# Graph attention on one core: building the kept keys with one-hot matmuls and picking flagged queries with multiply and add, in place of indirect transfers

## The chip, the cores and the metric

The kernel runs on one core of a Trainium2 chip. The metric is the device time in microseconds (us); the kernel before has a median of 13151.83 us over three runs (13146.24 to 13156.08). A core has these engines: PE (TensorE: matmul, with PEld its weight loads), DVE (VectorE), ACT (ScalarE), POOL (GpSimd) and SP (SyncE, which here only issues transfers). Each engine runs its own instructions strictly in the order written, and waits on semaphores for what others make.

## The reference, cut to what matters

Two layers on 3327 nodes with 128 features, with a sparse weighted adjacency matrix `adj` (about 0.12% of the entries plus the diagonal).

```python
# layer 0
x = layernorm(x + norm_rows(adj) @ x @ W_in + norm_rows(adj.T) @ x @ W_out)
# layer 1: d = 128 "heads" of h = 8 numbers each
q = (x @ Wq.T).reshape(d, n, h); k = ...; v = ...
a = einsum('dnh,dmh->dnm', q, k) * d**-0.5
a = a + adj + adj
a = softmax(a, axis=2)
out = einsum('dnm,dmh->dnh', a, v).reshape(n, h * d) @ Wo.T
x = layernorm(x + out)
```

So there are 128 attention maps of 3327 by 3327, each with only 8 numbers per query and key. The softmax needs, for every query of every head, a bound on its largest score.

## The kernel before, in words

**Stages.** Layer 0 takes until about 430 us of the span. The projections (L546 to L604) then write queries, keys and values of all heads to memory, with queries and keys split into bf16 parts, and the squared length of every key (`size_d`) and query (`reach_d`); they end at 1002 us. After a lead-in the main loop runs from 1097 to 12973 us, and a last phase (`last(joined)`) joins the parts, multiplies by Wo and normalizes.

**The main loop.** There are 32 groups of 4 heads (`GH`). A group walks over 7 blocks of up to 512 queries, and in each over 26 tiles of 128 keys. One step of this walk is called a half here: PE makes scores for one tile of keys, one block of queries and two heads (`e_ps`, L1156, two matmuls), ACT exponentiates all 1024 columns in one instruction (`es`, L1173; L1175 in the last, narrow block, for four heads at once), and, a step later, PE multiplies with the values (`o`, L1107). A group has 338 halves, the kernel 10,816. A program order written out by hand (a manual schedule for PE, ACT, DVE, Pool and SP) puts one piece of side work into each half. The two score banks `e_ps` and seven buffers `es` let PE and ACT run a little ahead of each other.

**Side work 1, the items.** The stream `maxima` yields items in a fixed order; the function `due(halves)` says how many must have been taken by a half, from a line drawn per group so that they are done `MARGIN` = 45 halves ahead of the next group's beginning. A half with an item is called busy. What the items find for group g + 1 while group g runs is the bound of each query's largest score:
- Only long keys can give a large score. For each head the 1024 longest keys (`TOP`), and the next 1024 up to `KEPT` = 2048, are compacted into `k_kept`, with their six bf16 part rows on partitions.
- `of_top(g, x)` (52 items for a pair of heads, x = 0 or 1): PE multiplies a tile of queries with 512 kept keys (L912) for both heads, DVE takes the maximum over the 512 (L921).
- `fix(g, x)` then compares, per query, the best found with query length times the longest key not looked at (`reach` from L711, L719). For each partition it lists up to `ROOM` = 8 queries that are not settled (`slots`), fetches their rows with 16 indirect gathers of 128 rows each on Pool's queue (L742), and splits them into bf16 parts on Pool.
- `of_rest(g, x)` (18 items) turns these rows (`slot_rows_q`, transposed by PE at L897) and multiplies them with the second 1024 kept keys. `merge` joins both maxima; `to_queries` turns the result (L868) and SP stores it (L871, L875) where the group's `q_e` loads read it.
- `turn()` moves the running `fix` and `merge` one step on, once per item.

**How the kept keys are built.** `select` finds, per head, the two length limits by halving, then ranks the keys with matmuls of ones and triangles, and computes for every key its place: 0 to 1023, 1024 to 2047, or a place behind all of these. `scatter` writes each group's 4 x 26 columns of 128 keys with one indirect transfer each (L518, 3328 in all, on Pool's queue, paced by the counter `load_of_pool`) into `kept_d`. `parts_of_kept` (L627 to L646) loads them back and splits them on Pool (`parts`, L640 to L645). Eight fill items per group transpose the parts on PE (L897, eight matmuls of 128 columns) and DVE casts them into `k_kept` (L906, 48 x 512).

**Side work 2, the neighbours (`beside`).** A half without an item, from the half `START` = 1536 on, runs one step of `neighbours()`. For each of 26 tiles of 128 nodes it makes the attention part of the nodes' own neighbours (up to 16 slots). K phase: for each slot a gather of 128 rows of all heads' keys (`near_rows`, L961, 4 KB a row, up to three ahead, four buffers), a product with the query on DVE in two halves (L996), a reduction (L999) and an addition. Then the softmax over the 16 slots: Pool subtracts the maximum (L1032), ACT exponentiates in four pieces (L1038), Pool multiplies by `gain` (L1041) and sums in four additions (L1043 to L1046). V phase: for each slot a gather, a product on DVE in two halves (`prod`, L1056), and Pool adds it to `acc` (L1062); a slot takes four steps. `prod` has two buffers that the K phase, the sums and the V phase share.

**Choices.** The selection of heads 0 to 3 and of 4 to 31 runs beside the projections, together with the scatters of group 0; the selections of the other heads run in halves without an item from `READY` = 310 on. The lead-in, before the first half, takes 8 fill items and 49 (`LEAD`) items of block maxima alone.

Of the kernel before, what the change touches and what calls it, by code (L numbers as in the profile page):

```python
# [11 lines left out]
U32 = mybir.dt.uint32  # L12
# [44 lines left out]
SLACK = 1.001  # L57
EARLY = [(0, 4), (4, 28)]
# [3 lines left out]
MARGIN = 45  # L62
# [7 lines left out]
def gnn_layers(ctx: ExitStack, tc: tile.TileContext, x, adj, adjt, w_in, w_out, wq, wk, wv, wo, out):  # L70
# [17 lines left out]
    nc.gpsimd.iota(order, pattern=[[-P, NT]], base=N - 1, channel_multiplier=-1)  # L88
    behind = const.tile([P, NT], F32, name="behind")
    nc.vector.tensor_copy(behind, order)  # L90
    every_f = const.tile([P, P], F32, name="every_f")
    nc.gpsimd.memset(every_f, 1.0)
    nothing = const.tile([1, HEADS], F32, name="nothing")
    nc.gpsimd.memset(nothing, 0.0)
# [3 lines left out]
    base_i = const.tile([P, 2, ROOM], I32, name="base_i")  # L98
    nc.gpsimd.iota(base_i, pattern=[[N, 2], [0, ROOM]], base=-P, channel_multiplier=1)
    query_base = const.tile([P, 2, ROOM], F32, name="query_base")  # L100
    nc.vector.tensor_copy(query_base, base_i)
# [25 lines left out]
    place_d = {  # L127
        first: dram.tile([P, n // GH, NT, GH], U32, name=f"place_d{first}") for first, n in EARLY + LATE
    }
    kept_d = [dram.tile([NP, H], F32, name=f"kept_d{h}") for h in range(HEADS)]  # L130
# [24 lines left out]
    with ExitStack() as c0:  # L155
# [145 lines left out]
        early = c_att.enter_context(tc.tile_pool(name="early", bufs=1))  # L301
        load = c_att.enter_context(tc.tile_pool(name="load", bufs=2))
# [87 lines left out]

        k_st = [with_ones(early.tile([P, 2, NP], BF16, name="k_st0"))]

        def select(pool, bank, first, n, tag=""):
# [3 lines left out]
            sizes = pool.tile([P, n, NT], F32, name=f"sizes{tag}")  # L397
# [4 lines left out]
            nc.sync.dma_start(sizes[P - 1 :, :, NT - 1], nothing[:, :n])  # L402
# [27 lines left out]
            for which, kept, bound in ((0, TOP, 3.3), (1, KEPT, 1.63)):  # L430
# [3 lines left out]
                for _ in range(HALVINGS):  # L434
# [4 lines left out]
                    nc.vector.tensor_scalar(few[:, 0], total, float(kept), None, op0=ALU.is_le)  # L439
                    nc.vector.tensor_scalar(few[:, 1], total, float(kept), None, op0=ALU.is_gt)  # L440
# [7 lines left out]
            for limit, to in ((0, top_least), (1, least)):  # L448
                nc.vector.tensor_scalar(to[:, first : first + n], limits[:, limit], SLACK, None, op0=ALU.mult)
            passed = [pool.tile([P, 2, n], BF16, name=f"passed{i}{tag}") for i in range(2)]  # L450
            nc.vector.memset(passed[0], 0.0)
            batch = min(NT, NB // n)
            by_tile = sizes.rearrange("p h t -> p t h")
            for t0 in range(0, NT, batch):
# [3 lines left out]
                masks = pool.tile([P, 2, nt, n], BF16, name=f"masks{tag}")  # L458
                for which in range(2):
                    nc.vector.tensor_tensor(  # L460
                        masks[:, which], by_tile[:, these], limits[:, which, None, :].to_broadcast(shape), op=ALU.is_gt
                    )
                    yield
                chosen = pool.tile([P, 2, nt, n], U32, name=f"chosen{tag}")
                nc.vector.tensor_copy(chosen[:, 0], masks[:, 0])
                nc.vector.tensor_sub(chosen[:, 1], masks[:, 1], masks[:, 0])
# [11 lines left out]
                ranks = [r.rearrange("p (t h) -> p t h", h=n) for r in ranks]  # L478
                second = pool.tile(shape, F32, name=f"second{tag}")
                place = pool.tile(shape, F32, name=f"place_of{tag}")  # L480
                nc.vector.tensor_tensor(second, leading[:, None, :].to_broadcast(shape), ranks[0], op=ALU.subtract)
                nc.vector.tensor_copy(place, ranks[0])
                yield
                nc.vector.tensor_add(second, second, ranks[1])
# [991 lines left out]
```

## Time and profile before

| | us |
|---|---|
| median of three runs | 13151.83 |
| the profiled execution | 13224.05 |
| its span | 13222.4 |
| PE busy in it | 11302.4 (85%) |
| ACT busy | 10990.5 (83%) |
| DVE busy | 9504.1 (72%) |
| POOL busy | 7295.3 (55%) |
| main loop with neighbours | 3094 to 10675 |
| main loop after them, with items | 10675 to 12638 |
| main loop without items | 12638 to 12973 |

A group line of the profile reads: line, engine, operation, output<-inputs, shapes, count | busy us, mean ns of one | idle time of the engine just before, and what ended it. A wait line reads: engine, instruction <- what it waited for: us in total, times, longest. An engine's busy share is an average over stages, so the stages are read one by one.

### The profile page before, as it was taken

The page shows a single profiled execution, that of the slowest core. Times are in us where ns is not written, and L with a number is a line of the kernel's source. Part 1 is how long each engine was busy: PE and PEld are TensorE (multiplying, and loading weights), DVE is VectorE, ACT ScalarE, POOL GpSimd, SP SyncE. Part 2 cuts the span into 40 slices and gives each one's busy share as a digit, 9 for nine tenths or more (in the row PEclk, how much of TensorE's full clock was granted, in tenths as well). Part 3 has the DMA queues.
Part 4 walks back from the last instruction along what each step waited for, and adds up shares of the span by engine and source line. Part 5 has one row for each costly group of instructions (what it writes and reads, how often), then busy time and mean ns, then how long its engine had stood idle before and what let it go on. Part 6 is the DMA issues. An engine that isn't in the chain of part 4 may idle for free.

```text
span 13222.4 us, 227945 instructions
## 1 busy us (share of the span) xinstructions
PE 11302.4 (85%) x84312; PEld 2645.3 (20%) x84312; DVE 9504.1 (72%) x16699; ACT 10990.5 (83%) x11667; POOL 7295.3 (55%) x6732
## 2 busy tenths in 40 slices
PE   7537877998898898888989889889899889999986
PEld 3211111211111111111111111111111112222114
DVE  9668877657887787777888778778887756555406
ACT  6444656898998899888899889889899889999993
POOL 0156444566776666666776677776666766111102
PEclk9767988999999999999999999999999999999997
DMA  6554344454555564545556655544565542111104
GB/s 234 160 147 52 28 31 32 33 38 66 83 86 75 80 86 75 77 76 78 83 84 82 76 80 82 82 80 79 82 80 79 79 39 21 17 16 17 13 7 122
DMA packets 3191887, 937.74 MB, mean 71 GB/s; under 512 B 2859821, under 2 KB 3041701, under 8 KB 3184103
## 3 DMA queue, kind: packets, MB, share of 16 engines
q1 hardware_dynamic: 2915559, 387.22, 29.1%
q0 software_dynamic: 270464, 489.31, 16.1%
q10 hardware_dynamic: 4736, 46.52, 1.0%
q8 instruction: 665, 10.90, 0.4%
q14 instruction: 463, 3.79, 0.1%
HBM read 779.88 MB, written 170.53 MB: 72 GB/s over the span
## 4 chain that ended last, share of the span: by engine, by line
ACT 30%; PE 26%; issue 14%; DVE 11%; DMA 8%; POOL 7%; SPq 5%; ACTq 0%; DVEq 0%; POOLq 0%
ACT es L1173 27%; PE o L1107 12%; PE e_ps L1156 8%; PE m L912 3%; POOL kept_d L518 3%; DVE mx_top L921 2%; DMA negmax_d<-turned 2%; ACT es L1175 2%; DMA kept_d<-keys,at 1%; POOL slot_q L742 1%; SPq L372 1%; DMA near_rows<-kn_d,near 1%; DMA q_e<-q_d 1%; PE acc L224 1%; SPq L401 1%
## 5 line engine op out<-in xcount | busy, mean ns | idle before, releaser
L1173 ACT ACTIVATE es<-e_ps 128x1024 f32<-128x1024 f32 (+1 forms) x9984 | 9502.6, 1025 | 1211.9 <-PE e_ps L1156 1003.0
L1107 PE MATMUL o<-es,v 128*9 128x512 f32 x46592 | 5873.8, 576 | 58.3 <-ACT es L1175 22.0
L921 DVE TENSOR_REDUCE mx_top<-m 128x1 f32<-128x512 f32 x6448 | 4134.1, 684 | 1742.1 <-PE m L912 1710.5
L1156 PE MATMUL e_ps<-q_e,k_st 50*128 50x512 bf16 (+1 forms) x23296 | 4270.3, 376 | 642.8 <-ACT es L1173 418.2
L518 POOL DMA_INDIRECT kept_d<-keys,at x3328 | 3572.8, 1074 | 1641.3 <-issue 929.2
L1156 PEld LDWEIGHTS <-k_st 50*128 50x128 bf16 (+1 forms) x23296 | 1272.6, 95 | 6919.9 <-issue 6610.5
L742 POOL DMA_INDIRECT slot_q<-qf_d,slot_rows x992 | 996.4, 1004 | 1633.6 <-DVE slot_rows L734 1337.7
L921 DVE TENSOR_REDUCE mx_rest<-m 128x1 f32<-128x512 f32 x1984 | 1271.4, 683 | 424.4 <-PE m L912 412.9
L912 PE MATMUL m<-k_kept,q_m 48*128 48x512 bf16 x6448 | 1365.2, 385 | 216.6 <-DVE mx_top L921 197.3
L1062 POOL TENSOR_TENSOR acc<-acc,prod 128x1024 f32<-128x1024 f32 x390 | 903.9, 2318 | 444.3 <-DVE prod L1056 379.5
L1107 PEld LDWEIGHTS o<-es,v 128*9 128x9 f32 x46592 | 695.4, 88 | 2198.3 <-issue 1805.5
L1175 ACT ACTIVATE es<-e_ps 128x1020 f32<-128x1020 f32 x832 | 837.3, 1022 | 166.6 <-PE e_ps L1156 143.2
L1056 DVE TENSOR_TENSOR prod<-near_rows,s 128x512 f32<-128x512 f32 x832 | 656.0, 797 | 2.7 <-POOL s L1041 1.6
L996 DVE TENSOR_TENSOR prod<-qn,near_rows 128x512 f32<-128x512 f32 x832 | 565.6, 689 | 67.5 <-DMA near_rows<-kn_d,near 67.5
L906 DVE CAST k_kept<-m 48x512 bf16<-48x512 f32 x512 | 352.7, 689 | 283.1 <-PE m L897 248.1
L999 DVE TENSOR_REDUCE s<-prod 128x64 f32<-128x512 f32 x832 | 553.0, 674 | 0.0
L961 POOL DMA_INDIRECT near_rows<-kn_d,near x416 | 425.4, 1023 | 185.1 <-issue 69.0
L912 PE MATMUL m<-k_kept,slot_rows_q 48*128 48x512 bf16 x1984 | 430.1, 383 | 108.0 <-DVE mx_rest L921 91.8
L961 POOL DMA_INDIRECT near_rows<-vn_d,near x416 | 436.7, 1050 | 118.2 <-issue 97.2
L224 PE MATMUL acc<-a_t,x 128*128 128x512 f32 (+1 forms) x728 | 311.2, 584 | 64.8 <-DMA a_t<-in_adj_dram 44.8
L912 PEld LDWEIGHTS <-q_m 48*128 48x128 bf16 x6448 | 336.5, 97 | 84.9 <-issue 66.1
L897 PE MATMUL m<-ident_b,parts 128*48 128x128 bf16 x2048 | 128.9, 241 | 233.6 <-POOL parts L645 158.1
(265 smaller groups left out, 5602.2 us busy)
## 6 DMA issues: line engine op xcount, KB each, us to landing
kept_d<-keys,at POOLq DMA_INDIRECT x3328
q_m<-q_d SPq DMA_DIRECT2D x744, 52.0 KB
q_e<-q_d SPq DMA_DIRECT2D x2304, 16.0 KB
a_t<-in_adj_dram ACTq DMA_DIRECT2D x13, 1663.5 KB
a_t<-in_adj_dram SPq DMA_DIRECT2D x13, 1663.5 KB
a_t<-in_adjt_dram SPq DMA_DIRECT2D x13, 1663.5 KB
a_t<-in_adjt_dram ACTq DMA_DIRECT2D x13, 1663.5 KB
q_d<-parts SPq DMA_DIRECT2D x13, 1536.0 KB
```

Of the source, the lines that this page charges most:

```text
L518: nc.gpsimd.indirect_dma_start(kept_d[s * GH + j], bass.IndirectOffsetOnAxis(ap=at[:n, t, j : j + 1], axis=0), keys[:n, j, t, :], None,)
L742: nc.gpsimd.indirect_dma_start(rows[:, y * ROOM + i, :], None, qf_d, bass.IndirectOffsetOnAxis(ap=at[:, y, i : i + 1], axis=0))
L912: nc.tensor.matmul(banks[y], of[rows[y], i * P : (i + 1) * P], kept[rows[y], x, c * NB : (c + 1) * NB], start=True, stop=True,)
L921: nc.vector.tensor_reduce(mx[:, n, j + y, c - c0 : c - c0 + 1], banks[y], axis=AX.X, op=ALU.max)
L961: nc.gpsimd.indirect_dma_start(rows.rearrange("p d h -> p (d h)"), None, table, bass.IndirectOffsetOnAxis(ap=near[:, t, i : i + 1], axis=0))
L996: nc.vector.tensor_mul(both[:, d], left[:, d], right[:, d])
L1056: nc.vector.tensor_mul(prod[:, d], vg[:, d], share[:, d])
L1062: nc.gpsimd.tensor_add(acc[:, :, :H], acc[:, :, :H], prod)
L1107: nc.tensor.matmul(o[32 * j : 32 * j + VW, :w], v4[:pt, j, t, :], e[j][:pt], start=t == 0, stop=t == NT - 1,)
L1156: nc.tensor.matmul(bank[:pt, y, x * NB // per : x * NB // per + w], k[r, x0 + x, t * P : t * P + pt], q[r, x0 + x, :w], start=True, stop=True,
L1173: nc.scalar.activation(es[:pt, :, :w], bank[:pt, :, :w], AF.Exp, scale=2.0)
L1175: nc.scalar.activation(es[:pt].rearrange(shape, x=per)[:, :, :, :w], bank[:pt].rearrange(shape, x=per)[:, :, :, :w], AF.Exp, scale=2.0,)
```

## The change

The kept keys are built without transfers. `select` no longer computes places but, for every key, its rank in its class relative to a window of `REACH` = 168 columns that is fixed for each of the 26 key columns t (`window(t)` = 1018 t / 26 - 72, rounded down): keys of the first class get a number in -168 to -1, those of the second in 0 to 167, others one far off. `rank_d` keeps it as fp32. For each column of 128 keys and each head, DVE compares the row -168 to 167 with that number (`hots_of`: a one-hot matrix of 128 x 336 in bf16), and PE multiplies the split keys with it into the window's columns of two open banks, one per class (`fill_piece`). The split is made on Pool from all 3328 keys of four heads (`split_keys`). Both banks are opened by a matmul with zeros and closed by one copy of 112 x 512 each on DVE. A group has 36 such items in place of 8. The limits are now found for 1024 keys in each class. A key whose rank falls outside its window sets `outside`, which joins the marks that lead to the general pass at the end; an unlucky input would need it.

`fix` now loads all queries of its two heads (`whole_q`, two loads of 128 x 26 x 8 numbers on SP, each ahead of that head's reach load). It makes `hits` (DVE, moved here from `merge`), and Pool picks the rows: four rounds of a product of 128 x 832 and six additions. The gathers are gone.

In the neighbours' V phase Pool makes the product in one piece as well as the addition; a slot takes two steps in place of four. `turn()` runs once in a half without an item (in every half in the first two groups). `MARGIN` is 60. Groups 0 and 1 are filled beside the projections, so the lead-in has 49 items and no fills. The pacing of Pool by `load_of_pool` has no scatters left to pace. `s` shares its room with the selection.

```diff
 def select(...):
...
+                nc.vector.scalar_tensor_tensor(
+                    at[0], whole, 0.5 * (REACH - 1) - NOWHERE, at[0], op0=ALU.mult, op1=ALU.add
                 )
...
+                nc.gpsimd.dma_start(rank_d[first][:, :, these], by_group)
-        def scatter(s, at, keys):
-
-            for t in range(NT):
-                n = P if t < NT - 1 else P - 1
-                for j in range(GH):
-                    nc.gpsimd.indirect_dma_start(
-                        kept_d[s * GH + j],
...
+        def split_keys(pool, keys):
+
+            keys = keys.rearrange("p j t h -> p (j t) h")
+            parts = pool.tile([P, GH * NT, len(QROWS), H], BF16, name="parts")
+            left = pool.tile([P, 4, NT, H], F32, name="slot_each").rearrange("p j t h -> p (j t) h")
+            nc.gpsimd.tensor_copy(parts[:, :, 0], keys)
+            nc.gpsimd.tensor_sub(left, keys, parts[:, :, 0])
...
+        def pieces_of_fill(x, u):
+            seen = [
+                t for t in range(NT) if window(t) < (u + 1) * NB and window(t) + REACH > u * NB
+            ]
+            return [seen[i : i + 2] for i in range(0, len(seen), 2)]
+
+        def hots_of(pool, at, x, piece):
+            made = {}
+            for t in piece:
+                for y in range(2):
+                    hot = made[t, y] = pool.tile([P, 2 * REACH], BF16, name="hot", bufs=8)
+                    nc.vector.tensor_scalar(hot, hot_no, at[:, t, 2 * x + y : 2 * x + y + 1], None, op0=ALU.is_equal)
+            return made
+
+        def fill_piece(banks, parts, hots, x, u, piece, last):
+            for t in piece:
+                lo, hi = max(window(t), u * NB), min(window(t) + REACH, (u + 1) * NB)
+                for which in range(2):
+                    for y in range(2):
+                        at = which * REACH + lo - window(t)
+                        nc.tensor.matmul(
+                            banks[which][64 * (1 - y) : 64 * (1 - y) + KR, lo - u * NB : hi - u * NB],
+                            parts[:, (2 * x + y) * NT + t].rearrange("p s h -> p (s h)"),
+                            hots[t, y][:, at : at + hi - lo],
+                            start=False,
+                            stop=last and t == piece[-1],
+                        )
+
+        def end_fill(banks, g, x, u):
+            for which in range(2):
+                c = which * TCUTS + u
+                nc.vector.tensor_copy(k_kept[g % 2][: 64 + KR, x, c * NB : (c + 1) * NB], banks[which][: 64 + KR, :])
+
+        def begin_fill(banks):
+            for which in range(2):
+                nc.tensor.matmul(banks[which], ident_b, nothing, start=True, stop=False)
...
 def fix(g, x, mx, found):
...
+                nc.sync.dma_start(whole_q[:, y], qf_d[at : at + NP].rearrange("(t p) h -> p t h", p=P))
                 nc.sync.dma_start(reach[:, y], reach_d[at : at + NP].rearrange("(t p) -> p t", p=P))
...
-                    nc.gpsimd.indirect_dma_start(
-                        rows[:, y * ROOM + i, :], None, qf_d, bass.IndirectOffsetOnAxis(ap=at[:, y, i : i + 1], axis=0)
...
+                for i in range(0, ROOM, 4):
+                    each = side.tile([P, 4, NT, H], F32, name="slot_each")
+                    shape = [P, 4, NT, H]
+                    nc.gpsimd.tensor_mul(
+                        each,
+                        hits[y][:, i : i + 4, :, None].to_broadcast(shape),
+                        whole_q[:, y, None].to_broadcast(shape),
                     )
+                    nc.gpsimd.tensor_add(each[:, :, :13], each[:, :, :13], each[:, :, 13:])
+                    nc.gpsimd.tensor_add(each[:, :, :6], each[:, :, :6], each[:, :, 6:12])
...
 def neighbours():
...
-                    for d in (slice(0, HEADS // 2), slice(HEADS // 2, HEADS)):
-                        nc.vector.tensor_mul(prod[:, d], vg[:, d], share[:, d])
-                        yield
-                    yield
                     if i == 0:
-                        nc.gpsimd.tensor_copy(acc[:, :, :H], prod)
+                        nc.gpsimd.tensor_mul(acc[:, :, :H], vg, share)
                     else:
+                        prod = side.tile([P, HEADS, H], F32, name="prod", bufs=2)
+                        nc.gpsimd.tensor_mul(prod, vg, share)
                         nc.gpsimd.tensor_add(acc[:, :, :H], acc[:, :, :H], prod)
+                    yield
                     transfer()
                     yield
...
 the main loop
...
+                            if not busy or g < 2:
+                                turn()
                             if not busy:
...
-                            if load_of_pool[0] < 0.88 * halves + 80 or len(scattered) < 2:
-                                spend(1.3)
-                                next(scattering, None)
```

## The prediction

> **What bounds the kernel now.** I read first the page's busy shares and the chain that ended last, then the busy time by stage for the tile es alone, then the waits and the groups of the longest stage. The columns of the stage table are the stretch, its length, and the busy time and count of PE, PEld and ACT, then the granted clock, the DMA share and GB/s; ACT's count is the number of halves.
>
> ```profile
> PE 11302.4 (85%) x84312; PEld 2645.3 (20%) x84312; DVE 9504.1 (72%) x16699; ACT 10990.5 (83%) x11667; POOL 7295.3 (55%) x6732
> ACT 30%; PE 26%; issue 14%; DVE 11%; DMA 8%; POOL 7%; SPq 5%; ACTq 0%; DVEq 0%; POOLq 0%
> ...
> 3094.00:10675.00 7581.00, 3792.77 (x30123) 449.54 (x30120) 6677.12 (x6986) 0.96 0.54 80
> 10675.00:12638.00 1963.00, 1040.82 (x8396) 125.21 (x8400) 1857.18 (x1951) 0.99 0.19 18
> 12638.00:12973.00 335.00, 184.66 (x1528) 22.68 (x1520) 328.01 (x346) 1.00 0.03 6
> ```
>
> No engine is bound by itself: one half costs 7581/6986 = 1.085 us while the neighbour work runs, 1963/1951 = 1.007 after it, 335/346 = 0.967 with neither neighbours nor maxima. So 0.967 is the floor of PE and ACT together, and the 0.12 us above it in the long stage, 820 us in all, is what the change can win or double. Which waits make it up (us in total, times, longest):
>
> ```profile
> ACT es L1173 <- PE e_ps L1156: 521.3, 748, 21.8
> POOL acc L1062 <- DVE prod L1056: 379.5, 187, 10.7
> PEld L897 <- POOL parts L645: 143.7, 20, 12.3
> PE m L897 <- POOL parts L645: 137.7, 20, 12.0
> DVE turned L868 <- DMA negmax_d<-turned: 74.5, 26, 10.2
> PE e_ps L1156 <- DMA negmax_d<-turned: 62.4, 15, 9.9
> DVE reach_of L719 <- DMA reach_of<-reach_d: 32.3, 4, 22.2
> ```
>
> ACT waits for scores because PE stands in order behind something else. I followed every idle time of ACT above 4 us in this stage back through its releasers: (a) PE waits for Pool's split of the kept keys, 20 times, 153 us; (b) PE waits at a group's start for the maxima that SP is still storing, 18 times, 119 us; smaller ones behind the reach and neighbour loads. Note the second line: today Pool waits for DVE in the V phase of the neighbours, not DVE for Pool.
>
> Rows of the same stage that price the edits (busy, mean ns):
>
> ```profile
> L518 POOL DMA_INDIRECT kept_d<-keys,at x2023 | 2203.8, 1089 | 1041.9 <-issue 554.7 <-DMA kept_d<-keys,at 349.7 <-DMA keys<-kf_d 122.7
> L1062 POOL TENSOR_TENSOR acc<-acc,prod 128x1024 f32<-128x1024 f32 x390 | 903.9, 2318 | 444.3 <-DVE prod L1056 379.5 <-DVE turned L868 49.5 <-DVE slot_at L732 8.8
> L742 POOL DMA_INDIRECT slot_q<-qf_d,slot_rows x656 | 668.9, 1020 | 256.4 <-issue 161.6 <-DVE slot_rows L734 55.8 <-DMA slot_q<-qf_d,slot_rows 12.4
> L1056 DVE TENSOR_TENSOR prod<-near_rows,s 128x512 f32<-128x512 f32 x832 | 656.0, 797 | 2.7 <-POOL s L1041 1.6 <-POOL acc L1062 1.1
> L961 POOL DMA_INDIRECT near_rows<-vn_d,near x416 | 436.7, 1050 | 118.2 <-issue 97.2 <-DVE prod L996 9.8 <-DVE mx_top L921 1.8
> L906 DVE CAST k_kept<-m 48x512 bf16<-48x512 f32 x320 | 220.5, 689 | 192.3 <-PE m L897 184.1
> L1032 POOL TENSOR_TENSOR s<-s,top 128x2048 f32<-128x2048 f32 x26 | 117.9, 4534 | 0.0
> L1041 POOL TENSOR_TENSOR s<-s,gain 128x2048 f32<-128x2048 f32 x26 | 94.6, 3637 | 139.7 <-ACT s L1038 139.5
> L1043 POOL TENSOR_TENSOR prod<-s 128x1024 f32<-128x1024 f32 x26 | 61.9, 2382 | 2.1
> ```
>
> **The change, part by part.** Sums go against the profiled execution, 13224 us, which lies 72 us (0.55%) above the median of 13151.8.
>
> *Pool loses and gains.* Gone: 3328 scatters (3573 us of busy Pool on the whole page) and 992 slot gathers (996). Added: 416 V products, 31 splits of [128,832] (cast 1.0, subtract 1.9 twice, copies 1.0 each, scaled from 677, 1169 and 611 ns at 512 columns: 9 to 10 us) and 62 picks. A pick has four rounds of one multiply of 832 (1.5 by L1041's rate, 1.8 by L1032's) and six shrinking adds (2.7, scaled from 1325, 892 and 582 ns at 512, 256 and 128), plus the existing small split: 19.5 us. Pool's total falls to about 5000. The total is not the question; the V phase is.
>
> *V phase.* A tile's V phase is now 16 slots of two turns each. In the changed program, built, 119 turns make a tile (151 before); a turn needs a half without an item, and items now take 176/338 = 0.521 of the halves (36 fill items a group in place of 8). So a tile takes 119/0.479 = 248 halves, and from its last softmax exponential to the next tile's first product on DVE there are 37 turns, 77 halves, at 1.02 us each 79 us. That product writes one of two prod buffers, and must wait for Pool's add of slot 14. Pool has to do until then: the four sums and the gain product 8.5 us (3.6 + 2.4 + 1.3 + 0.7 + 0.5, medians), 15 gathers at 1.05 + 0.2 issue = 18.7, one multiply M, 14 times M + 2.32. M is between 1.82 (half of L1041, a broadcast product as here) and 2.38 (L1043); I take 1.85, the nearer kind: 87 us, against 79: DVE waits 8 us per tile (16 at the upper end). Picks and splits queue on the same Pool: over 25 tiles some 9 picks and 6 splits fall into the stretch, 9 x 19.5 + 6 x 9.5 = 235 us, 9.4 per tile. Together 17 to 21 us in which DVE stands. Behind the waiting product stand the maxima reductions (L921); PE then runs out of m banks after two or three halves, and the scores stop. So all but 2 us reach ACT: 25 x 17 to 19 = 430. Bounds: 0 (Pool faster than its rows) and 800 (M at 2.38 and every pick in the stretch).
>
> *Waits that go.* The splits no longer hang on scattered rows read back, and come 18 items ahead of their fill; the group's maxima are due 60 halves ahead instead of 45. That the steps of fix and merge now run only in halves without an item changes little: 16 steps of a merge at 0.479 a half are 34 halves, before, one per item, 16/0.438 = 36. (a) and (b) are 272 us over 23 groups, 11.8 each; over the 19.1 groups with neighbours beside them: -225. Next late would be the reach load and Pool.
>
> *PE.* Per group 240 fill matmuls and 8 opening ones replace 64. Eight of the old took 0.63 us in one burst, 79 ns each: (240 - 64) x 0.079 + 8 x 0.38 (a 512-column product, L912's mean 384 ns) = 17 us per group. PE is busy 0.95 of a 1.007 us half, so little of it hides. Ends: 0 and 325 (17 x 19.1); taken 160, half, since halves with beside work have slack of about 0.1 us.
>
> *DVE.* Per group, 120 one-hots and 8 wide casts come, 16 casts and 1.36 groups' share of V products go: 26 x 32 x 0.797 = 663 us over 19.1 groups = 34.7. A one-hot is [128,336] bf16 by a column; nearest rows: a two-input compare of 208 columns 361 to 571 ns (L785), a scalar op of 128 columns 265 ns at the median (L1013). Ends 0.2 and 0.48; taken 0.27: 32 + 5.5 - 11 - 34.7 = -8 per group, -150 us of DVE, of which a third shows: -50 (ends -100, +200).
>
> *SP.* Each fix loads two whole_q tiles in 32-byte pieces, 3328 each, ahead of the reach loads: 124 more issues, 128 kept loads gone. One reach load with as many pieces holds SP 0.45 us and the second 2.0 to 2.6 us, 13.6 at most. The q_e and negmax loads queue behind. The picks, some six steps (12 halves) after the issue, wait on Pool for these loads; gathers and V adds stand behind them. For both +30 (0 to 150: 13.6 us in 11 of the 41 fixes that fall there).
>
> *Ends.* Projections: one-hots for two groups (some 70 us of DVE plus the range checks) against 128 scatters: 0 (-40 to +40). Lead-in: eight key items (11.5 us) and part of the 22 us idle of DVE before them go: -20. Halves up to 1536: denser items +20 (-60 to +100). Neighbours end 526 halves sooner, at 1.025 rather than 1.092: -35. The 1950 halves after carry the extra fills at 0.02: +40.
>
> Sum: 430 - 225 + 160 - 50 + 30 + 0 - 20 + 20 - 35 + 40 = +350: 13,574 profiled, 13,500 as a median.
>
> *Rules weighed.* The row first: Pool's L1032 takes 4534 ns for 2048 columns. The Trainium skill, "GPSIMD Engine Reference", §3.1 Elementwise, gives 4497 ns for a tensor_tensor add of that size, so trace and page agree; §4.1 Engine selection of that page speaks against this change: a two-input product belongs on VectorE, GpSimd being about twice as slow. By that rate M would be 2.25, the tile's wait 14 rather than 8 us, and the whole +500. Here the trace has the broadcast product L1041 at 3637 ns, and the sum goes by it.
>
> **Rivals.** (1) *Pool keeps up*, and the kernel is faster. Place: the first product after each V phase. For it: in the trace Pool idles 380 us waiting for DVE's products, and its total falls by 2300 us. Against it: 5.4 us per slot against 4.2 halves. Without the 430 the sum is -80: 13,070. It decides once the wait is below 3 us per tile, which needs M near 1.3 and the picks out of the stretch. (2) *Pool keeps up and PE's fills hide*: -80 - 160 - 30 = -270: 12,880. Against it PE's 85%. (3) *PE and DVE become the bound*: fills unhidden and one-hots at their upper end, 350 + 165 + 250 = +765: 13,840. For it: the waits of DVE for m (L912) total 936 us in the long stage, so PE's queue is already late. (4) *The range check rejects the data* and the general pass runs as well. The check allows 84 ranks from a tile's centre; on these inputs the farthest lies 71.5 away, so it should not.
>
> **How the numbers follow.** Forecast 0.57, (1) 0.19, (2) 0.07, (3) 0.16, (4) 0.01. Range 12,930 to 14,050: it leaves out most of (2) and the ends where M is 2.38 and fills don't hide at once (0.08). The forecast's own range is 13,250 to 13,800. 0.2% (26 us) is about what a measurement of this kernel tells from no change; (1) reaches into it: faster 0.21, same 0.04, slower 0.75.
>
> **What would show it.** After each V phase DVE waiting for Pool's add, some 15 us, 25 times, and an ACT idle time to match; the waits of PE for Pool's split gone; halves of the stage at about 1.13 us, of the stretch after it near 1.03; Pool's product near 1.85 us; one-hots near 0.27. I am wrong if the product is near 1.3, if Pool's adds end before DVE comes, or if PE waits elsewhere for the fills.

## The result and the profile after

The changed kernel takes 13911.03 us (median of four runs, 13907.55 to 13925.9), the kernel before 13153.95 beside it: a ratio of 1.058, with a 95% interval of 1.056 to 1.060. The profiled execution has a span of 13911.3 us, 689 more than before. The direction came as forecast and the range of 12,930 to 14,050 held the time; the forecast's own range, 13,250 to 13,800, did not, and the slowdown is 5.8% where 13,500 would have been 2.6%.

One fact has to stand ahead of the experiments: in all four later sessions, each on another chip, the same kernel before took 15,929 to 16,096 us, while the changed kernel took 13,982 and 13,983 on the two where it ran. So there the change is a gain of 13%. The verdict of this section holds for the first pair of runs; variants of the changed kernel are compared with the changed kernel. What slows the kernel before there is taken up with the runs.

The page of the changed kernel, busy shares and the chain that ended last:

```profile
PE 11771.5 (85%) x90200; PEld 2855.8 (21%) x90200; DVE 10081.0 (72%) x19451; ACT 11023.2 (79%) x11667; POOL 4716.9 (34%) x4564
PE 35%; ACT 16%; POOL 16%; DVE 15%; issue 10%; DMA 4%; SPq 4%; ACTq 0%; DVEq 0%; POOLq 0%
```

Pool has lost a third of its work, yet its share of the chain has more than doubled, from 7% to 16%. The stages by the tile es (stretch, length, PE, PEld and ACT busy with counts, clock, DMA share, GB/s): with neighbours, after them, without items:

```profile
3110.00:10797.00 7687.00, 3561.72 (x27921) 416.33 (x27921) 6222.94 (x6487) 0.94 0.48 77
10797.00:13182.00 2385.00, 1235.03 (x9984) 148.33 (x9984) 2210.05 (x2314) 0.99 0.18 18
13182.00:13662.00 480.00, 264.15 (x2188) 32.62 (x2184) 467.45 (x494) 1.00 0.03 6
```

A half costs 7687/6487 = 1.185 us with neighbours (1.085 before), then 1.031 (1963/1951 = 1.006 before), then 0.972 (335/346 = 0.968). The loss lies in the stage with neighbours. Its waits, from 3100 to 10,980 us (us in total, times, longest):

```profile
ACT es L1222 <- PE e_ps L1205: 1189.3, 1074, 37.8
...
DVE prod L1050 <- POOL acc L1111: 396.2, 22, 36.0
...
PE m L579 <- DVE hot L570: 298.8, 125, 34.9
...
DVE reach_of L772 <- DMA reach_of<-reach_d: 121.7, 21, 29.7
...
DVE prod L1050 <- DMA near_rows<-kn_d,near: 87.6, 17, 12.2
...
DVE turned L917 <- DMA negmax_d<-turned: 24.2, 10, 6.0
```

The waits for Pool's split are gone, those for the maxima have shrunk. In their place DVE waits for Pool's last addition, 18 us each time, PE waits for one-hots, and the reach load is late four times as long as before. One of the lags, in the timeline (start, length, instruction, idle time before):

```profile
3433.66 1.98 POOL L1110 TENSOR_TENSOR prod<-near_rows,s 128x1024 f32<-128x1024 f32 x1
3435.72 2.27 POOL L1111 TENSOR_TENSOR acc<-acc,prod 128x1024 f32<-128x1024 f32 x1
3438.02 0.69 DVE L1050 TENSOR_TENSOR prod<-qn 128x512 f32<-128x512 f32 x1 [26.74 <-POOL acc L1111]
...
3441.64 2.42 POOL L1111 TENSOR_TENSOR acc<-acc,prod 128x1024 f32<-128x1024 f32 x1
...
3441.81 2.79 DVE L1050 TENSOR_TENSOR prod<-qn 128x512 f32<-128x512 f32 x1
...
3444.85 1.94 ACT L1222 ACTIVATE es<-e_ps 128x1024 f32<-128x1024 f32 x2 [29.88 <-PE e_ps L1205]
```

DVE stood 26.7 us for the addition, ACT 29.9 us behind it. The row at 3441.81 shows a second thing: a product that takes 0.69 us takes 2.79 beside Pool's addition and ends 0.5 us after it. The one-hots, in groups 5 to 23, beside the neighbours, and in the stretch after them:

```profile
L570 DVE TENSOR_SCALAR hot<-hot_no,at 128x336 bf16<-128x336 bf16 x2280 | 910.2, 463 | 119.1 <-PE m L579 118.4
```

```profile
L570 DVE TENSOR_SCALAR hot<-hot_no,at 128x336 bf16<-128x336 bf16 x720 | 170.7, 302 | 138.7 <-PE m L579 138.4
```

Without Pool's arithmetic beside it a one-hot takes 302 ns; with it, 463 on the mean. (The records of successive one-hots overlap, so the busy time of one is less: 170.7/720 = 0.24 us after the neighbours, 910.2/2280 = 0.40 beside them.) Of the 2280, 194 take over half a microsecond; 190 of these end less than half a microsecond behind the end of a Pool instruction, 141 of them behind the V phase's product or addition. What the 190 take above 299 ns sums to 367 us.

To place the 671 us that groups 5 to 23 lost (366.5 us per group before, 401.8 after), the idle times of ACT in these 19 groups were followed back through their releasers to their first cause:

| idle ACT, us, first cause | before | after | difference | forecast |
|---|---|---|---|---|
| Pool's addition (the lag) | 0 | 409 | +409 | +430 |
| Pool's split, maxima, q_e | 298 | 68 | -230 | -225 |
| one-hots 194, maxima reductions 129, all others 370 | 393 | 693 | +300 | +110 (PE +160, DVE -50) |
| reach load | 36 | 148 | +112 | +30 |
| neighbours' rows (K phase) | 37 | 87 | +50 | 0 |

Together +641. The rows overlap a little: they add up to 764 and 1405 us, where all idle time of ACT in these groups is 739 and 1384, so a row is good to some 25 us, and the split within the third row to some 40. The kernel before has no one-hots here.

### The profile page after: what moved, and what is told of

Same layout as the page of the kernel before. It is cut to its first block, busy times and chain, and to the rows that moved or that the text cites. A ratio compares the mean times of both kernels' runs of the same rounds, so it can differ in the third digit from the quotient of the medians.

```text
span 13911.3 us, 241167 instructions
## 1 busy us (share of the span) xinstructions
PE 11771.5 (85%) x90200; PEld 2855.8 (21%) x90200; DVE 10081.0 (72%) x19451; ACT 11023.2 (79%) x11667; POOL 4716.9 (34%) x4564
## 4 chain that ended last, share of the span: by engine, by line
PE 35%; ACT 16%; POOL 16%; DVE 15%; issue 10%; DMA 4%; SPq 4%; ACTq 0%; DVEq 0%; POOLq 0%
PE o L1156 16%; ACT es L1222 13%; PE e_ps L1205 10%; POOL acc L1111 4%; POOL prod L1110 4%; PE m L975 4%; DVE mx_top L984 3%; ACT es L1224 2%; POOL near_rows L1015 2%; DVE mx_rest L984 2%; DVE hot L570 2%; PE m L579 2%; POOL slot_each L799 1%; DMA reach_of<-reach_d 1%; DVE prod L1050 1%
## 5 line engine op out<-in xcount | busy, mean ns | idle before, releaser
L975 PE MATMUL m<-k_kept,q_m 48*128 48x512 bf16 x6448 | 1412.1, 383 | 408.7 <-DVE mx_top L984 392.5
L799 POOL TENSOR_TENSOR slot_each<-hits,whole_q 128x832 f32<-128x832 f32 x248 | 416.3, 1679 | 3678.8 <-DVE hits L787 2828.3
L570 DVE TENSOR_SCALAR hot<-hot_no,at 128x336 bf16<-128x336 bf16 x3840 | 1281.5, 398 | 313.2 <-PE m L579 309.5
L1110 POOL TENSOR_TENSOR prod<-near_rows,s 128x1024 f32<-128x1024 f32 x390 | 772.6, 1981 | 14.7 <-DMA near_rows<-vn_d,near 8.2
L579 PE MATMUL m<-hot,parts 128*48 128x168 bf16 (+11 forms) x7200 | 463.5, 235 | 326.4 <-DVE hot L570 325.0
L1050 DVE TENSOR_TENSOR prod<-qn,near_rows 128x512 f32<-128x512 f32 x832 | 619.4, 744 | 94.4 <-DMA near_rows<-kn_d,near 87.6
L975 PE MATMUL m<-k_kept,slot_rows_q 48*128 48x512 bf16 x1984 | 466.9, 391 | 256.9 <-DVE mx_rest L984 254.7
L1053 DVE TENSOR_REDUCE s<-prod 128x64 f32<-128x512 f32 x832 | 559.6, 673 | 0.0
L579 PEld LDWEIGHTS <-parts 128*48 128x48 bf16 x7680 | 283.8, 104 | 707.7 <-issue 669.5
L590 DVE CAST k_kept<-m 112x512 bf16<-112x512 f32 x240 | 154.5, 685 | 300.0 <-PE m L579 299.9
```

Of the source, the lines that this page charges most:

```text
L570: nc.vector.tensor_scalar(hot, hot_no, at[:, t, 2 * x + y : 2 * x + y + 1], None, op0=ALU.is_equal)
L579: nc.tensor.matmul(banks[which][64 * (1 - y) : 64 * (1 - y) + KR, lo - u * NB : hi - u * NB], parts[:, (2 * x + y) * NT + t].rearrange("p ...
L975: nc.tensor.matmul(banks[y], of[rows[y], i * P : (i + 1) * P], kept[rows[y], x, c * NB : (c + 1) * NB], start=True, stop=True,)
L1050: nc.vector.tensor_mul(both[:, d], left[:, d], right[:, d])
L1110: nc.gpsimd.tensor_mul(prod, vg, share)
```

## The experiments

**1. Which of Pool's parts costs: the product undone, or only given time.**

The run e1 has the V phase of the kernel before:

```diff
...
+                    for d in (slice(0, HEADS // 2), slice(HEADS // 2, HEADS)):
+                        nc.vector.tensor_mul(prod[:, d], vg[:, d], share[:, d])
+                        yield
+                    yield
...
-                        nc.gpsimd.tensor_mul(prod, vg, share)
...
```

The run e2, and again g2, has three turns per slot:

```diff
                     transfer()
                     yield
+                    yield
```

> The changed kernel with one part undone: the neighbours' V product is on DVE again, in two halves, and a slot takes four steps. Theory (the product costs twice on Pool: DVE stands about 409 us for Pool's last addition of each V phase, and one-hots that meet a Pool product or addition stand until it ends, 372 us of DVE): the wait of DVE's first product for Pool's addition falls from 389 to under 40 us, the mean one-hot of the stage with neighbours from 463 to about 390 ns; 663 us of products come back to DVE, of which about 200 show; 13,911 - 409 - 100 + 200 = 13,600. Rival (the added fills and one-hots are simply more work for DVE and PE, and the wait for Pool only moves to another place): DVE is fuller than before, so no gain, 13,850 or more.

> The changed kernel with one step more per V slot (three in place of two), the product staying on Pool. Theory (a lag: 5.5 us of Pool work per slot against 4.2 halves): with 6.3 halves per slot Pool keeps up but for picks and splits, the wait of DVE for Pool's addition falls from 389 to under 100 us, the time to about 13,911 - 310 = 13,600; the one-hots stay as slow as they are (463 ns in the stage), since Pool does the same products. Rival (Pool's work itself is what costs, wherever it lies): no less than 13,850.

Measured: e1 13,549 us and e2 13,781; for both 13,600 was expected. e2 ran on another chip than the changed kernel so far, so it was taken again beside it:

> The changed kernel as the reference of the two runs beside it: 13,900 to 14,000 us.

> Three turns per V slot again, now beside the changed kernel on the same chip. Theory (the lag goes, but while it lasted nothing else could wait, and the one-hots that meet Pool's products now wait more): 150 to 200 us less than the changed kernel, under half of the 409. Rival (the lag is worth its whole length, and the chip hid it): 350 to 400 us less.

13,983 and 13,781: 202 us less. Waits and one-hots of the changed kernel (g1), then of g2, from 3300 to 11,550 us:

```profile
DVE prod L1050 <- POOL acc L1111: 399.2, 21, 36.0
...
DVE reach_of L772 <- DMA reach_of<-reach_d: 164.5, 25, 36.1
```

```profile
L570 DVE TENSOR_SCALAR hot<-hot_no,at 128x336 bf16<-128x336 bf16 x2520 | 968.3, 450 | 165.5 <-PE m L579 163.4 <-PE e_ps L1205 1.3 <-issue 0.3
```

```profile
DVE reach_of L772 <- DMA reach_of<-reach_d: 220.0, 27, 22.4
...
DVE prod L1050 <- POOL acc L1111: 48.3, 8, 10.2
```

```profile
L570 DVE TENSOR_SCALAR hot<-hot_no,at 128x336 bf16<-128x336 bf16 x2520 | 1116.4, 510 | 140.7 <-PE m L579 137.8 <-PE e_ps L1206 2.7
```

The lag is as good as gone (399 to 48 us of DVE), but one-hots rose from 450 to 510 ns and the reach wait from 165 to 220. That fits the theory of g2: while DVE stood for the lag, these could not be late. Half of the lag's length was a gain. With the product on DVE (e1) the lag is gone too, though the products then wait 111 us for Pool's additions, and the one-hots fall to 366:

```profile
L570 DVE TENSOR_SCALAR hot<-hot_no,at 128x336 bf16<-128x336 bf16 x2880 | 870.1, 366 | 163.1 <-PE m L579 158.9 <-PE e_ps L1207 1.4 <-remote 1.1
```

So 663 us of products less on DVE made the kernel slower: e1 and e2, both without the lag and on one chip, differ by 232 us in favour of the fuller DVE.

**2. Why one-hots are slow.**

The run e4 interleaves the one-hots of two heads:

```diff
+                pair = pool.tile([P, 2 * REACH, 2], BF16, name="hot", bufs=4)
...
-                    hot = made[t, y] = pool.tile([P, 2 * REACH], BF16, name="hot", bufs=8)
+                    hot = made[t, y] = pair[:, :, y]
```

The run f4 has a second comparison behind each one-hot:

```diff
...
+                    nc.vector.tensor_scalar(spare, hot_no, 5.0, None, op0=ALU.is_equal)
```

> The changed kernel with the one-hots of two heads interleaved, so that each is written (and read by PE) at every other element. Theory (the one-hots run in a fast mode that cannot run beside a Pool instruction on SBUF operands; at every other element they leave that mode): a one-hot takes about 410 ns everywhere, in place of 301 without Pool beside it and 463 with; hardly any ends together with a Pool instruction, 0.2 us or less of the 372 us of prolonging in place of all; the time within 100 us of 13,911, since the slower form takes back what the waits give. Rival (they are slow in that stage for another reason): slower in both stages by the same 110 ns or not at all, with the prolonged ones still there.

14,211 us, and the theory fell. Beside the neighbours and after them:

```profile
L571 DVE TENSOR_SCALAR hot<-hot_no,at 128x336 bf16<-128x336 bf16 x2280 | 1302.1, 655 | 52.2 <-PE m L580 50.6
```

```profile
L571 DVE TENSOR_SCALAR hot<-hot_no,at 128x336 bf16<-128x336 bf16 x720 | 237.7, 415 | 80.4 <-PE m L580 79.8
```

At every other element a one-hot takes 415 ns in the stretch after the neighbours and 655 beside them; that is 548 us of prolonging, not none.

> The changed kernel with a second comparison behind each one-hot, of the same shape and type but with a constant in place of the number read from SBUF, into a tile that nobody reads. Theory (a one-hot waits for Pool because it reads a second operand, the column of numbers, and not because of its speed): the second comparison takes about 300 ns on the mean in the stage with neighbours, next to 460 of the first, and never ends together with a Pool instruction. Rival (any comparison in a fast form waits for Pool): both are prolonged alike. 3840 x 0.30 = 1150 us more of DVE, of which a third to a half shows: 14,350 to 14,550.

14,259 us, a little under the 14,350 to 14,550 expected. In the stage with neighbours:

```profile
L570 DVE TENSOR_SCALAR hot<-hot_no,at 128x336 bf16<-128x336 bf16 x2280 | 1192.1, 523 | 27.5 <-PE m L581 27.3
...
L572 DVE TENSOR_SCALAR spare<-hot_no 128x336 bf16<-128x336 bf16 x2280 | 573.2, 251 | 0.0
```

The comparison with a constant takes 251 ns in this stage and 240 after it; 4 of 2280 end with a V-phase product or addition of Pool, against 204 of those that read their number from SBUF. That looks as if only the form that reads a column beside its tile waited. The trace shows otherwise: the constant form stands directly behind a one-hot, which has mostly waited in its place, so it rarely meets Pool; where it does, it waits as well. 43 of them began while a two-input Pool instruction ran, and 39 of these ended behind it, by about 0.1 us, as the one-hots do. The longest, in the timeline:

```profile
4251.42 0.45 DVE L570 TENSOR_SCALAR hot<-hot_no,at 128x336 bf16<-128x336 bf16 x1
4251.64 4.52 POOL L1087 TENSOR_TENSOR s<-s,top 128x2048 f32<-128x2048 f32 x1
4251.79 4.48 DVE L572 TENSOR_SCALAR spare<-hot_no 128x336 bf16<-128x336 bf16 x1
```

So all three forms of the comparison wait for Pool: dense with a column, dense with a constant, and at every other element with a column (e4). Not every DVE instruction does. In the changed kernel the reduction `s<-prod` (L1053), which reads SBUF too, began 90 times beside a two-input Pool instruction and took 671 ns there, 673 elsewhere; and in f4 the multiplication by a constant `negative<-most` (fp32, read in runs of four) did so 6 times and took 255 ns, against 260.

The Trainium skill, "SBUF — State Buffer", section "SBUF: two separate sides", says that DVE and GpSimd take one pair of ports in turn, each for a whole instruction, and that a DVE instruction needs this pair if it has two SBUF inputs, against a GpSimd instruction that reads SBUF, or if it runs in a mode that uses two ports. The product at 3441.81 agrees with the first condition (0.69 to 2.79 us). The comparison with a constant has one SBUF input, so by that section it must have run in such a mode; the trace does not tell modes. The one-hot of e4 agrees if its column counts as an input, which the section doesn't say.

**3. Taking Pool out of the V phase, and the reach loads.**

The run e3, and again g3, issues both reach loads first:

```diff
-                nc.sync.dma_start(whole_q[:, y], qf_d[at : at + NP].rearrange("(t p) h -> p t h", p=P))
                 nc.sync.dma_start(reach[:, y], reach_d[at : at + NP].rearrange("(t p) -> p t", p=P))
+            for y in range(2):
+                at = (g * GH + 2 * x + y) * N
+                nc.sync.dma_start(whole_q[:, y], qf_d[at : at + NP].rearrange("(t p) h -> p t h", p=P))
```

f1 is e1 and e3 together; f2 is f1 with the addition on DVE as well:

```diff
-                        nc.gpsimd.tensor_add(acc[:, :, :H], acc[:, :, :H], prod)
...
+                            nc.vector.tensor_add(acc[:, d, :H], acc[:, d, :H], prod[:, d])
```

> The changed kernel with the two reach loads issued ahead of the two loads of whole_q, instead of between and behind them. Theory (DVE's wait for the reach load, 122 us in the stage with neighbours and 148 us of idle ACT, comes from standing behind whole_q on SP): the wait falls to about 35 us, as in the kernel before, and the time by about 110, to 13,800. Rival (the reach loads are late because of all that SP and the queues carry): the wait stays near 120 us, 13,900.

> The reach loads first again, beside the changed kernel on the same chip. Theory (a wait of its own, worth its length): 90 to 120 us less than the changed kernel, as the pair with the V product on DVE had it (13,549 and 13,445 on two chips). Rival (DVE's next wait takes most of it over): 30 us less.

13,881 us, then 13,871 beside the changed kernel's 13,983: 112 less. The wait for the reach load in g3, 65 us in place of the 165 of g1:

```profile
DVE reach_of L774 <- DMA reach_of<-reach_d: 65.3, 11, 32.0
```

The load was late because it stood behind whole_q.

> The changed kernel with the V product on DVE again and the reach loads ahead of whole_q: the two reversals that gained, together. Theory (they touch different waits): 13,549 less the 100 that reach still cost there, 13,450, with DVE's wait for the reach load under 35 us in place of 123. Rival (behind the reach load stands another wait of the same length): 13,550.

> As the run beside it, with the V addition on DVE as well, so that in the V phase Pool only issues gathers, besides picks and splits. Theory (one-hots are slow only where they meet a Pool product or addition): the mean one-hot of the stage with neighbours falls from 366 ns to 325 or less, against 301 where Pool is idle, though DVE is fuller than in any other run. 574 us of additions come to DVE, of which a third shows, less 40 for the one-hots: 13,450 + 150 = 13,600. Rival (one-hots are slow because DVE or its reads from SBUF are crowded): 366 ns or more.

13,445 and 13,292 us on one chip. One-hots of f2 in the stage with neighbours:

```profile
L570 DVE TENSOR_SCALAR hot<-hot_no,at 128x336 bf16<-128x336 bf16 x3000 | 771.4, 319 | 187.3 <-PE m L579 183.0 <-PE e_ps L1211 3.4
```

319 ns as expected, but the time was forecast to rise by 150 and fell by 152, though DVE took 580 us of additions: in f1 DVE's products still wait 114 us for Pool's addition, which f2 doesn't have:

```profile
DVE prod L1110 <- POOL acc L1116: 113.7, 25, 8.4
```

A half of f2's stage costs 8844/8203 = 1.078 us. f2 beats the changed kernel by 4.9% across chips (13,292 against 13,983), and the kernel before on the chip it ran on (15,929); against the first pair's 13,154 it would be 1% slower.

**4. The picks, and the order alone.**

The run e8 undoes the picks:

```diff
-                    nc.gpsimd.tensor_mul(
-                        each,
-                        hits[y][:, i : i + 4, :, None].to_broadcast(shape),
-                        whole_q[:, y, None].to_broadcast(shape),
-                    )
...
+                    nc.gpsimd.indirect_dma_start(
+                        rows[:, y * ROOM + i, :], None, qf_d, bass.IndirectOffsetOnAxis(ap=at[:, y, i : i + 1], axis=0)
+                    )
```

The run e7 is the kernel before with the two moves in order alone:

```diff
-MARGIN = 45
+MARGIN = 60
...
+                    of_kept = begin_kept(g + 1)
                 yield from of_top(g, 1)
                 if g + 1 < NG:
                     maxima_of(g + 1, 1)
-                    of_kept = begin_kept(g + 1)
+                    parts = split(of_kept)
                 yield from of_rest(g, 0)
...
-                    yield from fills(g + 1, split(of_kept))
+                    yield from fills(g + 1, parts)
```

> The changed kernel with the picks undone: the flagged queries' rows come by 16 indirect gathers again, whole_q is not loaded. Theory (whole_q makes the reach load late, 148 us of idle ACT, and picks hold Pool and thereby the neighbours' gathers, 87 us): both fall to about 40, and the lag of the V phase changes little, since 16 gathers take about 17 us of Pool where a pick took 19.5: 13,911 - 150 = 13,760. Rival (picks are cheap, and gathers bring the long waits of Pool for transfers back): 13,900 or more.

> The kernel before with scatters, gathers and DVE's product as they are, and only the two moves in order that the change also makes: the kept keys are loaded ahead of of_top(g, 1) and split ahead of of_rest(g, 0), and MARGIN is 60. Theory (the 295 us of idle ACT behind the split and the group's maxima were a matter of order, not of the scatters): PE's wait for the split under 20 us in place of 144, the waits for the maxima about halved, 13,152 - 230 = 12,920. Rival (the scatters themselves make the split late): the wait moves to Pool's copies waiting for kept rows, with 16 items standing behind them, 13,100 or more.

Both were missed. e8 took 14,489 us, 507 more than the changed kernel on the same chip; the reach wait did fall (147 to 70 us), but 314 us of ACT waits appeared whose end no record explains, where the changed kernel has 4; with the picks undone 992 small gathers are back, and part 5 finds the same waits beside small transfers. e7 took 16,195 us against 16,072, 0.7% slower, where 12,920 was expected. In its trace PE and its weight loads wait for Pool's split 2 times, in place of 23 in the kernel before on that chip, so the order does remove that wait; what it is worth can't be read there, since other stalls fill the time. That the 230 us of the table are owed to order rather than to the missing scatters stays open.

**5. What slows the kernel before on these chips.**

> The kernel before, unchanged, profiled once more, because beside the four runs above it took 16,070 us (granted clock 0.855) and not 13,152 (0.936), while the variants of the changed kernel lay where they should. Theory (its 4320 scatters and slot gathers on Pool's queue are sometimes slower, and everything paced by them waits): where it takes 16,000 us, the mean scatter is over 1.3 us in place of 1.07, or the waits of Pool for its own transfers are over 1000 us, and ACT waits for what hangs on the kept keys. Rival (the whole chip or its clock was slower): all matmuls and the exponentials take longer in the same proportion. If it takes 13,150 us here, it says nothing on either.

> The changed kernel, unchanged, on the same chip as the run beside it. Theory: 13,911 us within 0.3% wherever it runs, as it has no scatters. Rival (the other state is one of the chip): slower by as much as the kernel before.

> The changed kernel with 3328 further scatters of 128 rows of 32 bytes on Pool's queue, one in every third half, into tensors that nobody reads and from rows that never change. Theory (on the chips where the kernel before takes 16,070 us, small indirect transfers in dense succession hold up PE by themselves): ACT's waits that no record explains, 4 us in the unchanged kernel, come to several hundred us, and the time is 14,500 or more. Rival (what hangs on the scattered rows made the kernel before slow there): Pool has the room, nothing waits, 14,100 or less.

The run f3 is the changed kernel with scatters of constant rows:

```diff
...
+                            if halves % 3 == 0 and halves < 3 * 3328:
+                                nc.gpsimd.indirect_dma_start(
+                                    idle_d[halves // 3 % 8],
+                                    bass.IndirectOffsetOnAxis(ap=row_no[:, :1], axis=0),
+                                    idle_rows,
+                                    None,
+                                )
```

The kernel before took 16,087 us, the changed one 13,982 on the same chip, 0.5% over its first time. In the kernel before there, the scatter's issue takes 1059 ns, not more than before (1074), so the first theory's form of it is wrong. Its rival, a slower chip or clock, falls too: the last group, without items, takes 326.1 us in both traces. New are waits whose end no instruction in the record explains (whole run, waits of e5):

```profile
ACT es L1173 <- remote: 1925.0, 357, 33.4
...
DVE mx_top L921 <- remote: 818.2, 152, 51.1
```

The trace of the first pair's kernel before has none. Between 1322 and 1356 us, for example, Pool issues a scatter every 1.27 us, and one pair of PE's score matmuls gives its signal 29 us after it began. A half's cost in us, in stretches of 20 us from the first half on, by the number of small indirect transfers (scatters and slot gathers) that Pool issued in them:

| issues in 20 us | 0 | 1-3 | 4-7 | 8-11 | 12-19 |
|---|---|---|---|---|---|
| before, first pair | 1.03 | 1.16 | 1.11 | 1.11 | 1.10 |
| before, e5 | 1.07 | 1.17 | 1.24 | 1.58 | 4.37 |

A stalled stretch also collects issues, so the table alone proves no direction. f3 does: 3328 scatters of constant rows that nothing waits for made the changed kernel slower by 2,850 us across chips, to 16,832, 0.86 us each. In its stage with neighbours, 3300 to 12,500 us:

```profile
DVE prod L1057 <- POOL acc L1118: 1085.2, 28, 65.1
...
ACT es L1229 <- remote: 505.5, 146, 11.3
```

Part of the loss is the lag, for Pool issues the scatters in the V phase too: DVE waits 1,085 us for Pool's last addition in place of 396. The stretch after the neighbours shows the scatters without the lag. Groups 24 to 28 take 473 us each in place of the changed kernel's 346 (g1), 1.1 us for each of their 113 scatters. From 13,200 to 16,000 us Pool stands idle for 1,782 us waiting for the next flagged queries, and ACT's unexplained waits are 599 us, most of that loss. So dense small transfers on Pool's queue hold up PE there by themselves. By what, was not found: the packets of the instruction queue took 1.20 us on the mean in the first pair's trace and 1.21 in e5's, and of e5's 240 unexplained waits over 3 us only 18 ended within 2.5 us of one. Whether it is the chip or something else that changed between the first session and the later ones is not shown either, for the two changed together, and f3 has no run beside the first pair.

## Why the prediction was right in direction and wrong in size

- **The lag** of the V phase, forecast at 430 us, is 409: 22 waits of 18 us. Pool's product took 1.98 us where 1.85 was taken, the pick 4 x 4.7 + 2.4 = 21.2 rather than 19.5. The mechanism, the place and the size were right. That it is worth its full length was wrong: given time (g2), the lag's end returns 202 us.
- **The waits that go** were right in size: -230 against -225. The 272 us had been spread over 23 groups, though the stage has 6986/338 = 20.7; with these the forecast would be -251. Which part of the change does it, the order or the missing scatters, stays open (e7).
- **The step that failed is DVE's**, the cost of a one-hot in the stage with neighbours. It was taken at 0.27 us everywhere. In the stretch after the neighbours, without Pool's arithmetic, that was nearly right: a one-hot takes 0.30, and a half costs 1.022 us in groups 24 to 29 against 1.000 in groups 26 to 29 before, 0.022 more where 0.02 was taken. But beside the neighbours one-hots wait for Pool's two-input instructions, of which the change doubles the V phase's, and take 463 ns. DVE and PE together, forecast at 160 - 50 = 110 us, came to 300, and 194 us of ACT's idle time has a one-hot as its first cause. The relief of DVE was booked as a gain, and the runs show the reverse: giving the product back to DVE saves 434 us (e1 against the changed kernel's 13,983, on two chips; 232 of it where the lag is gone anyway), the addition 152 more. The warning stood in a row that the prediction used. It gave L785 as 361 to 571 ns; these are its means after the neighbours and beside them, and the sum made nothing of the difference:

```profile
L785 DVE TENSOR_TENSOR hits<-slots,tile_no 128x208 f32<-128x208 f32 x82 | 46.9, 571 | 0.0
```

```profile
L785 DVE TENSOR_TENSOR hits<-slots,tile_no 128x208 f32<-128x208 f32 x24 | 8.7, 361 | 0.0
```

- **SP's step** was bounded rightly (0 to 150) and taken at 30 instead of 112, though the text itself had the whole_q loads ahead of the reach loads; g3 gives 112 back.
- **Missing** was the gathers' delay behind picks on Pool: 50 us.
- The ends: lead -23 (-20), the first five groups +55 (+20), the earlier end of the neighbours -48 in groups 24 and 25 (-35), the stretch after +32 (+40). With 671 these give 687, against 350.
- Of the rivals, (1) and (2) fell: Pool's product is 1.98 us, not 1.3. (3) came nearest in time. Its sum was added up wrongly: 13,152 + 765 is 13,917, not 13,840. That it lies 6 us from the measured time is luck, for its mechanism, one-hots slow by themselves and fills that hide nowhere, is not what the runs show: one-hots take 0.30 us, far from 0.48, where nothing blocks them, and after the neighbours fills and one-hots cost what was taken. (4) shows no sign: the last phase is as long as before.
- That the sign turns in later sessions was in no case of the forecast. Nothing in the first trace speaks of it: there a half costs no more with dense scatters (1.10 us) than with few (1.16).

## What to carry to other kernels

Total busy time of an engine says little when a phase has its own pace: compare the work per step with the steps per step, and look for the buffer that closes the loop. Before moving work from DVE to Pool, look at which DVE instructions run beside it: here products and comparisons waited for nearly every two-input Pool instruction that they met, and reductions did not. So the move can cost the engine that it was meant to relieve. A wait that stands in the place of others is worth less than its length.

## What was not expected of the hardware

- A comparison of 336 columns with a number read per partition took 302 ns alone and 463 to 523 on the mean beside Pool's two-input arithmetic. With a constant it took 240 alone, and up to 4.48 us where it met a Pool instruction (39 of 43 waited). A reduction from SBUF took 671 ns beside Pool and 673 without.
- The kernel with 4320 small indirect transfers took 13,154 us in the first pair and 15,929 to 16,096 in the four later sessions; the kernel without them 13,911 and 13,982. 3328 transfers that nobody needs cost 2,850 us there, across chips.
